# A graph layer on one core: x of blocks and own messages made ahead, rows stored in three half passes, SyncE in program order and fetching one unit in 90

## Chip, core and metric

The kernel runs on one core of a Trainium2 chip. The metric is device time in microseconds (us) of one execution; the time before is the median of three runs. One further execution was profiled; its trace is where every duration below comes from. The engines are called as the profile calls them: PE (matmul) with PEld (its weight load), DVE, ACT, POOL (GpSimd) and SP (SyncE, which here only starts DMAs). L302 is line 302 of the kernel before.

## What is computed

One layer of a graph network on 50,000 nodes of 160 features and 1,650,000 edges, sorted by target. Every node has an edge to itself (`_loop`). In the reference, cut to what matters:

```
src = concatenate([_s, _d, arange(50000)]); dst = concatenate([_d, _s, arange(50000)])   # then sorted by dst, stable
ss, vv = s[src], v[src]                       # gather rows of x by edge
m = (four products of ss, vv with the edge's 4 attributes and W1..W5)
m_agg = segment_sum(m, dst)
h = (m_agg times Ws and Wv)
x = layernorm(x + (x + relu(h)))
```

Since everything up to the ReLU is linear in x for fixed attributes, the kernel sums attribute times x row per target first (four sums of 160 numbers per node, one for each attribute) and multiplies by the combined weights (`BWa`, `BWb`) afterwards.

## The kernel before, in words

**Tiling.** 128 edges are a *unit*, 6 units a *group*, 2 groups a *pair* (12 units), 20 groups a *super-group* (10 pairs). There are 2,086 groups, so 1,043 pairs. The main loop (L755) runs over pairs. For a unit, POOL gathers the 128 rows of x that its edges name (L302, one indirect DMA into a slice of `xg`; the tile `xg` holds a pair's 12 units, and the pool `rows` has 5 such tiles). DVE makes `hot` (which of 32 target slots an edge belongs to, L311) and `ha` (`hot` times each of the four attributes, L314), and PE multiplies `ha` by the gathered rows, accumulating a group in PSUM (L324). ACT copies the sums out (L327).

**After a chunk of 4 groups** (2 pairs) the sums are transposed (`turn`, L559, L562), multiplied by the weights (`apply_weights`, L573) and kept as `hp` (L577). When the last chunk that touches a block of 128 nodes is done, the block is finished: `nodes` loads the block's x and self sums (L589, L593), `own` makes the messages of the nodes to themselves (L607 to L620), `block` adds the chunks' parts (L630, L631), then the layer norm (L175 to L190) and the store (L734). These steps are put off by a fixed number of pairs with `after_pair` (L779 to L786): turn 1, weights and loads 2, own 3, block 4, square root 5, norm 6, send 7.

**Packing.** Self edges needn't be gathered, so from group 60 on (`HEAD`) the kernel reads edges from which they were taken out. It takes them out itself, beside the main loop: the edges are read in packs of 120 rows of 790 edges (`pack`, 17 packs), each row is compacted on DVE (L425 to L504; its self edges' attributes are summed into `mine`, L465), and each row is stored to DRAM by SP, one DMA for its edges (18 KB) and one for its self sums, at addresses held in a table (`row_table`) and loaded into SP registers, ten rows a step (`store`, L513 to L541, loads at L519 and L522). A row's tail is overwritten by the head of the next, so all rows are stored without their head of 32 entries and then all heads: 2 x 12 steps. From super-group 3 on the edges are loaded back from there (L238). The steps of a pack are spread evenly over the pairs up to its due time (L748 to L777), which is pair 19 for the first pack, 69 for the second, and 60 pairs later for each further one.

**Order.** The program is written in this order and a scheduler orders each engine's instructions by its own model, adding the waits. Instructions of an engine, SP's DMAs too, then run in that order. Every DMA of SP signals one of eight semaphores in turn and waits for the one that used it eight DMAs before.

**Fetching by rows.** The kernel has a second way to get a unit's rows, `fetch` (L656), which is empty before since `HELP` is: an engine loads 32 row offsets (`offsets`, made by ACT in `cast`, L258) into registers and starts one DMA of 640 bytes for each, four such batches a unit, at pairs about 7, 5, 4 and 2 ahead of its use. The unit is the last of its pair, and POOL then leaves it out (L301).

Of the kernel before, what the change touches and what calls it, by code (L numbers as in the profile page):

```python
# [38 lines left out]
F32 = mybir.dt.float32  # L39
# [12 lines left out]
NK = 4  # L52
# [14 lines left out]
HELP = {}  # L67
HEAD = 60
# [31 lines left out]
def tile_gnn_resnorm(ctx: ExitStack, tc: tile.TileContext, x, src, dst, attr, W1, W2, W3, W4, W5, Ws, Wv, out, n_edges):  # L100
# [110 lines left out]
    with tc.tile_pool(name="once", bufs=1) as once, tc.tile_pool(name="raw", bufs=2) as rawp, \  # L211
            tc.tile_pool(name="idx", bufs=2) as idxp, tc.tile_pool(name="rows", bufs=5) as rowp, \
            tc.tile_pool(name="far", bufs=3) as farp, \
            tc.tile_pool(name="ops", bufs=3) as op, tc.tile_pool(name="sums", bufs=4) as sump, \
            tc.tile_pool(name="hp", bufs=alive + 4) as hpp, tc.tile_pool(name="node", bufs=3) as np_, \
            tc.tile_pool(name="psC", bufs=1, space=PSUM) as psC, tc.tile_pool(name="psK", bufs=2, space=PSUM) as psK, \
# [10 lines left out]
        dq = nc.sync  # L227
        offsets = {}
# [20 lines left out]
        def cast(loaded):  # L249
            s, n, ri, sf, df, af = loaded  # L250
            if ri is not None:
                rf = rawp.tile([P, 2, P], F32, name="rf")
                nc.scalar.copy(rf[:n], ri[:n])
                sf, df = rf[:n, 0, :], rf[:n, 1, :]
            if HELP:

                ro = rawp.tile([P, P], I32, name="ro")
                nc.scalar.mul(ro[:n], sf, 4.0 * D)  # L258
                offsets[s] = ro
            return s, n, sf, df, af  # L260

        def place(cast_):

            s, n, sf, df, af = cast_
            ng = n // G

            first = idxp.tile([P, SG], F32, name="first")
            nc.vector.tensor_scalar(first[:n], starts[:n], df[:, 0:1], None, op0=ALU.mult)
            nc.tensor.matmul(bank[:, 3, :ng], ones[:n], first[:n, :ng], start=True, stop=True)
            gs = slice(s * SG, s * SG + ng)  # L270
            nc.vector.tensor_scalar(baseB[:, gs], bank[:, 3, :ng], float(N - 1), None, op0=ALU.min)
            for g in range(QG):
                r = slice(g * W, (g + 1) * W)
                for c0, c1, h in ((s * SG // QG, (s * SG + ng) // QG, g),
                                  ((s * SG + ng) // QG, math.ceil((s * SG + ng) / QG), min(g, ng % QG - 1))):
                    if c0 < c1:
                        nc.vector.tensor_scalar(rowid[r, c0:c1],
                                                baseB[r, c0 * QG:c1 * QG].rearrange("p (c g) -> p c g", g=QG)[:, :, h],
                                                pidx[r], float(-g * W), op0=ALU.add, op1=ALU.add)
            pi = bank[:, 1:3, :]  # L280
            nc.tensor.transpose(pi[:, 0, :n], sf, ident[:n, :n])
            nc.tensor.transpose(pi[:, 1, :n], df, ident[:n, :n])
            pk = psK.tile([P, NK, P], F32, name="pk")
            for k in range(NK):
                nc.tensor.transpose(pk[:, k, :n], af[:, :, k], ident[:n, :n])  # L285
            si = idxp.tile([P, P], I32, name="si")
            nc.vector.tensor_scalar(si[:, :n], pi[:, 0, :n], 0.0, float(N - 1), op0=ALU.max, op1=ALU.min)
            rel = idxp.tile([P, P], F32, name="rel")

            nc.vector.scalar_tensor_tensor(  # L290
                rel[:, :n].rearrange("p (g j) -> p g j", j=G), pi[:, 1, :n].rearrange("p (g j) -> p g j", j=G),
                float(N - 1), baseB[:, gs].unsqueeze(2).to_broadcast([P, ng, G]),
                op0=ALU.min, op1=ALU.subtract)
            nc.vector.tensor_reduce(extremes[:, 0, s:s + 1], rel[:, :n], axis=AX.X, op=ALU.min)
            nc.vector.tensor_reduce(extremes[:, 1, s:s + 1], rel[:, :n], axis=AX.X, op=ALU.max)
            return si, rel, pk
# [53 lines left out]
        def row_table(tmp):  # L350

            NT = npacks * RP
            ti = once.tile([1, NT], I32, name="ti")
            at = tmp.tile([1, NT], F32, name="at")
            node = tmp.tile([1, NT], F32, name="node")
            nc.vector.memset(ti, 0)
            with nc.allow_non_contiguous_dma(reason="one number of each row"):
                dq.dma_start(ti[:, :NR], dst[EH:EH + NR * L].rearrange("(o r e) -> o r e", o=1, e=L)[:, :, 0])
            nc.gpsimd.iota(at, pattern=[[L, NT]], base=0, channel_multiplier=0, allow_small_or_imprecise_dtypes=True)
            most, least = math.ceil(EH / degree) + FAR, max(math.floor(EH / degree) - FAR, 0)  # L360
            nc.vector.tensor_scalar(node, ti, float(N), float(-most), op0=ALU.min, op1=ALU.add)
# [5 lines left out]
            nc.vector.tensor_copy(moved.bitcast(I32), node)  # L367
            nc.vector.tensor_copy(node, moved.bitcast(I32))
# [3 lines left out]
            nc.vector.tensor_scalar(moved, ti, float(N), None, op0=ALU.min)  # L372
            nc.vector.tensor_tensor(moved[:, :NR], moved[:, :NR], node[:, :NR], op=ALU.subtract)
            nc.vector.tensor_reduce(strayed[0:1, 0:1], moved[:, :NR], axis=AX.X, op=ALU.min)
            nc.vector.tensor_reduce(strayed[0:1, 1:2], moved[:, :NR], axis=AX.X, op=ALU.max)
            by_round = "o (c i j) -> o c j i"
            nc.vector.tensor_scalar(ti.rearrange("o (c j i) -> o c j i", c=npacks, j=RS),
                                    at.rearrange(by_round, c=npacks, j=RS), float(4 * C), None, op0=ALU.mult)
            nodes_at = moved.bitcast(I32)
            nc.vector.tensor_scalar(nodes_at.rearrange("o (c j i) -> o c j i", c=npacks, j=RS),  # L380
                                    node.rearrange(by_round, c=npacks, j=RS), float(4 * NK), None, op0=ALU.mult)
            return ti, nodes_at

        def pack(c):
# [128 lines left out]
            def store(head, j):  # L513

                m = len(range(j, n, RS))
                if not m:
                    return
                i0 = r0 + j * (RP // RS)
                _, at = nc.values_load_multi_w_load_instructions(  # L519
                    row_at[0:1, i0:i0 + m], engines=[ET.SP], min_val=0, max_val=row_start(NR - 1)[0][1] * 4 * C,  # L520
                    skip_runtime_bounds_check_because="held within bounds")
                _, node = nc.values_load_multi_w_load_instructions(  # L522
                    node_at[0:1, i0:i0 + m], engines=[ET.SP], min_val=0, max_val=row_start(NR - 1)[1][1] * 4 * NK,
                    skip_runtime_bounds_check_because="held within bounds")
                for i in range(m):
                    p = j + i * RS
                    (lo, hi), (nlo, nhi) = row_start(r0 + p)
                    v = nc.s_assert_within(at[i], lo * 4 * C, hi * 4 * C,
                                           skip_runtime_bounds_check_because="held within bounds")
                    e = slice(0, W) if head else slice(W, L)  # L530
                    put(edge_bytes, v, e, C, T["rows"][p:p + 1, e, :])
                    if r0 + p < real:
                        v = nc.s_assert_within(node[i], nlo * 4 * NK, nhi * 4 * NK,
                                               skip_runtime_bounds_check_because="held within bounds")
                        e = slice(0, W // 2) if head else slice(W // 2, W)
                        put(self_bytes, v, e, NK, T["mine"][p:p + 1, 0, e, :])

            def put(mem, at, e, width, what):
                size = (e.stop - e.start) * width * 4
                dq.dma_start(mem[e.start * width * 4:][ds(at, size)].rearrange("(o f) -> o f", o=1),  # L540
                             what.bitcast(U8).rearrange("p e c -> p (e c)"))  # L541
# [4 lines left out]
            for head in (False, True):  # L546
                steps += [partial(store, head, j) for j in range(RS)]
# [36 lines left out]
        def nodes(b):  # L584

            nb, row = rows_of(b)
            cs = of_block[b]
            xt = np_.tile([P, D], F32, name="xt")
# [3 lines left out]
            sa = np_.tile([P, NK], F32, name="sa")  # L592
            dq.dma_start(sa[:nb], selves[0, row.start * NK:row.stop * NK].rearrange("(n k) -> n k", k=NK))  # L593
            rr = np_.tile([P, alive], F32, name="rr")
# [4 lines left out]
            return xt, sa, hot2  # L599

        def own(b, xt, sa, hot2):
# [7 lines left out]
            t = np_.tile([P, D], F32, name="t")  # L609
# [12 lines left out]
            return xt, t, hot2  # L622
# [55 lines left out]
        placed = {0: place(cast(load(0)))}  # L678

        strayed = once.tile([P, 2], F32, name="strayed")  # L680
        nc.vector.memset(strayed, 0.0)
        moved = once.tile([1, npacks * RP], F32, name="moved")
        with tc.tile_pool(name="begin", bufs=1) as beginp:
            row_at, node_at = row_table(beginp)
            weights(beginp, psM)
        packp = later_pools.enter_context(tc.tile_pool(name="pack", bufs=1))
        limit = once.tile([P, 1], F32, name="limit")
        nc.vector.memset(limit, float(KM))
        place_ = once.tile([P, L], F32, name="place")
        nc.gpsimd.iota(place_, pattern=[[1, L]], base=0, channel_multiplier=0, allow_small_or_imprecise_dtypes=True)  # L690
        nc.vector.tensor_scalar(place_, place_, degree, None, op0=ALU.add)
# [6 lines left out]
        nc.vector.memset(counts[:, 1], float(W))  # L698

        nz = math.ceil((row_start(0)[1][1] + W) / P)  # L700
        zeros = once.tile([P, nz * NK], F32, name="zeros")
        nc.vector.memset(zeros, 0.0)
        dq.dma_start(selves[0, 0:P * nz * NK].rearrange("(p f) -> p f", p=P), zeros)
# [11 lines left out]
        def do_weights(c):  # L715
            hps[c] = apply_weights(*parts.pop(c))
            for b in after[c]:
                of_nodes[b] = nodes(b)
# [22 lines left out]

        raws, has = {}, {}
# [11 lines left out]
        done, began = 0, 0  # L754
        for p, (s, g, ng) in enumerate(pairs):  # L755
# [13 lines left out]
            if packs:  # L769
# [8 lines left out]
            if (g + ng) % QG == 0 or g + ng == NG:  # L778
                after_pair(p + 1, do_turn, c, sums)  # L779
                for b in after[c]:  # L780
                    after_pair(p + 3, do_own, b)
# [3 lines left out]
                    after_pair(p + 7, do_send, b)  # L785
# [197 lines left out]
```

## Time and profile before

| what | us |
|---|---|
| median of three runs | 21079.56 |
| lowest, highest | 21071.74, 21093.23 |
| the profiled execution, whole | 16054.09 |
| its span, first to last instruction | 16052.3 |
| POOL busy / PE busy / DVE busy / ACT busy in it | 11845.4 / 12359.3 / 6413.6 / 1574.3 |
| mean granted PE clock in it | 0.687 of full speed |
| gathers: number, mean duration | 12516, 0.946 |
| SP: DMAs that store rows (L540) | 8128 |

The profiled execution is shorter than the timed ones by 5,025 us. The profile is of one execution; a row such as "L302 POOL DMA_INDIRECT xg<-in_x,si x12516 | busy, mean ns | idle before <-who ended it" stands for all instructions of one line. "issue" as the one who ended an idle means that nothing in the profile was waited for. An engine's busy time leaves out the starting of DMAs, so SP has none; its instructions are seen in the timeline and under their lines.

### The profile page before, as it was taken

The page shows a single profiled execution, that of the slowest core. Times are in us where ns is not written, and L with a number is a line of the kernel's source. Part 1 is how long each engine was busy: PE and PEld are TensorE (multiplying, and loading weights), DVE is VectorE, ACT ScalarE, POOL GpSimd, SP SyncE. Part 2 cuts the span into 40 slices and gives each one's busy share as a digit, 9 for nine tenths or more (in the row PEclk, how much of TensorE's full clock was granted, in tenths as well). Part 3 has the DMA queues.
Part 4 walks back from the last instruction along what each step waited for, and adds up shares of the span by engine and source line. Part 5 has one row for each costly group of instructions (what it writes and reads, how often), then busy time and mean ns, then how long its engine had stood idle before and what let it go on. Part 6 is the DMA issues. An engine that isn't in the chain of part 4 may idle for free.

```text
span 16052.3 us, 155475 instructions
## 1 busy us (share of the span) xinstructions
PE 12359.3 (77%) x47011; PEld 8724.9 (54%) x47012; DVE 6413.6 (40%) x15105; ACT 1574.3 (10%) x3873; POOL 11845.4 (74%) x12530
## 2 busy tenths in 40 slices
PE   6176877787777877787778777787878777787887
PEld 4155555555555555555555555555555555555555
DVE  4353434343443434353444434343444434353222
ACT  0011010010101010010101010010101010010100
POOL 7277777777777777777777777777777777777776
PEclk6576667666766667676766667677776766676766
DMA  2133333333333333333333333333333332332322
GB/s 72 34 76 79 77 81 76 79 75 82 75 79 77 78 80 76 80 74 81 75 81 77 78 79 77 80 76 78 75 81 77 78 78 74 77 76 76 75 72 63
DMA packets 813417, 1218.18 MB, mean 76 GB/s; under 512 B 288531, under 2 KB 591540, under 8 KB 808506
## 3 DMA queue, kind: packets, MB, share of 16 engines
q0 software_dynamic: 600768, 1026.11, 26.2%
q1 hardware_dynamic: 211196, 181.54, 4.1%
q8 instruction: 373, 6.11, 0.2%
q14 instruction: 472, 3.87, 0.1%
q10 hardware_dynamic: 608, 0.55, 0.0%
HBM read 1135.43 MB, written 71.86 MB: 75 GB/s over the span
## 4 chain that ended last, share of the span: by engine, by line
POOL 46%; issue 21%; PE 16%; DMA 13%; SPq 3%; DVE 1%; ACT 0%; POOLq 0%; DVEq 0%; ACTq 0%
POOL xg L302 46%; DMA xg<-in_x,si 13%; PE ps L324 7%; PE yx L614 3%; PE yx L613 2%; SPq L540 2%; PE pt L559 2%; PE phb L630 1%; PE phc L573 1%; SPq L522 1%; SPq L519 1%; PE ptx L607 0%; DVE pra L465 0%; DVE prow L504 0%; PE pk L285 0%
## 5 line engine op out<-in xcount | busy, mean ns | idle before, releaser
L302 POOL DMA_INDIRECT xg<-in_x,si x12516 | 11841.1, 946 | 4157.0 <-issue 3561.3
L324 PE MATMUL ps<-xg,ha 128*128 128x160 f32 x25032 | 7383.7, 423 | 3146.7 <-DMA xg<-in_x,si 3097.5
L324 PEld LDWEIGHTS ps<-xg,ha 128*128 128x128 f32 x25032 | 4989.1, 254 | 5478.5 <-DMA xg<-in_x,si 4913.8
L314 DVE TENSOR_TENSOR ha<-hot,pk 128x1536 f32<-128x1536 f32 x1043 | 1826.8, 1752 | 5367.2 <-PE ps L324 5367.2
L465 DVE SCALAR_TENSOR_TENSOR pra<-marks,prow 120x236 bf16<-120x236 f32 (+40 forms) x2924 | 1501.6, 514 | 33.1
L327 ACT COPY A<-ps 128x320 f32<-128x320 f32 x1043 | 443.4, 425 | 6528.1 <-PE ps L324 6503.8
L614 PE MATMUL yx<-BWb,xT 32*128 32x320 f32 x1564 | 1000.3, 735 | 1.6 <-ACT xT L608 1.6
L613 PE MATMUL yx<-BWa,xT 128*128 128x320 f32 x1564 | 960.8, 713 | 0.7 <-ACT xT L608 0.7
L559 PE MATMUL pt<-ident,A 128*128 128x128 f32 (+1 forms) x4172 | 918.2, 371 | 42.8 <-DVE t L620 30.2
L562 ACT COPY at<-pt 128x512 f32<-128x512 f32 (+1 forms) x1044 | 601.4, 580 | 3218.1 <-PE pt L559 3203.9
L630 PE MATMUL phb<-hp,hot 128*128 128x160 f32 x4688 | 892.6, 352 | 0.0
L630 PEld LDWEIGHTS phb<-hp,hot 128*128 128x128 f32 x4688 | 846.6, 236 | 14.9 <-ACT at L562 10.9
L573 PE MATMUL phc<-BWa,at 128*128 128x160 f32 x4176 | 790.9, 341 | 1.0 <-ACT at L562 1.0
L573 PE MATMUL phc<-BWb,at 32*128 32x160 f32 x4176 | 771.4, 327 | 0.0
L559 PEld LDWEIGHTS pt<-ident,A 128*128 128x128 f32 (+1 forms) x4172 | 642.7, 166 | 230.2 <-issue 114.3
L573 PEld LDWEIGHTS phc<-BWa,at 128*128 128x128 f32 x4176 | 736.2, 227 | 7.1 <-ACT at L562 6.6
L573 PEld LDWEIGHTS phc<-BWb,at 32*128 32x128 f32 x4176 | 636.9, 201 | 104.7 <-issue 104.7
L614 PEld LDWEIGHTS yx<-BWb,xT 32*128 32x128 f32 x1564 | 351.3, 278 | 605.7 <-ACT xT L608 300.7
L618 DVE TENSOR_SCALAR t<-yx,sa 128x160 f32<-128x160 f32 x391 | 149.7, 383 | 1193.5 <-PE yx L614 1192.5
L631 DVE TENSOR_TENSOR phb<-phb,t 128x160 f32<-128x160 f32 x391 | 129.8, 332 | 1168.3 <-PE phb L630 972.5
L620 DVE SCALAR_TENSOR_TENSOR t<-yx,sa,t 128x160 f32<-128x160 f32 x1173 | 445.0, 379 | 329.1 <-PE yx L614 323.3
L311 DVE TENSOR_TENSOR hot<-bank,rel 128x384 f32<-128x384 f32 x1043 | 564.1, 546 | 3.5
(148 smaller groups left out, 4547.5 us busy)
## 6 DMA issues: line engine op xcount, KB each, us to landing
xg<-in_x,si POOLq DMA_INDIRECT x12516
selves<-mine SPq DMA_DIRECT2D x4062, 0.2 KB
r<-edges SPq DMA_DIRECT2D x101, 360.0 KB
edges<-prow SPq DMA_DIRECT2D x2033, 17.8 KB
edges<-prow SPq DMA_DIRECT2D x2033, 0.8 KB
xt<-in_x SPq DMA_DIRECT2D x390, 80.0 KB
out<-o SPq DMA_DIRECT2D x390, 80.0 KB
pra<-in_attr SPq DMA_DIRECT2D x16, 1481.2 KB
```

Source lines behind the costliest of these rows:

```text
L302: nc.gpsimd.indirect_dma_start(out=xg[:, j, :], out_offset=None, in_=x, in_offset=bass.IndirectOffsetOnAxis(ap=placed[0][:, u + j:u + j + ...
L311: nc.vector.tensor_tensor(hot[:, :n], slotsP[:, 0:W].unsqueeze(1).to_broadcast([P, n, W]), rel[:, u:u + n].unsqueeze(2).to_broadcast([P, n ...
L314: nc.vector.tensor_tensor(ha[:, :n], hot[:, :n].unsqueeze(2).to_broadcast([P, n, NK, W]), pk[:, :, u:u + n].rearrange("p k u -> p u k").un ...
L324: nc.tensor.matmul(ps[:, j // G, :], ha[:, j].rearrange("p k w -> p (k w)"), xr, start=j % G == 0, stop=j % G == G - 1)
L465: nc.vector.scalar_tensor_tensor(T["waste"][:n, w0:w1], T["marks"][:n, w0 - a:w1 - a], float(w + 1), T["rows"][:n, w0:w1, 2 + k], op0=ALU. ...
L559: nc.tensor.transpose(pt[:f1 - f0, g, :], A[:, i, f0:f1], ident)
L562: evict(at[:, :, :ng].rearrange("f k g w -> f g k w"), pt[:f1 - f0, :ng].rearrange("f g (k w) -> f g k w", w=W))
L573: nc.tensor.matmul(ph[:ng * W], at[:, k, :ng].rearrange("f g w -> f (g w)"), bw[:, k, :], start=i == 0, stop=i == 2 * NK - 1)
L613: nc.tensor.matmul(y[:nb], xT[:, 0, :nb], BWa[:, ks, :], start=True, stop=False)
L614: nc.tensor.matmul(y[:nb], xT[:D - P, 1, :nb], BWb[:, ks, :], start=False, stop=True)
L620: nc.vector.scalar_tensor_tensor(t[:nb], y[:nb, i], sa[:nb, k:k + 1], t[:nb], op0=ALU.mult, op1=ALU.add)
L630: nc.tensor.matmul(ph[:nb], hot2[:r, i, :nb], hp[:r], start=i == 0, stop=i == len(cs) - 1)
```

## The change

1. `HELP` gets SP with a period of 90 units: SP fetches one unit in 90 by rows. ACT makes the offsets of every super-group.
2. `HEAD` goes from 60 to 100 groups, so five super-groups are read unpacked. There are 2,087 groups then and 1,994 rows, still 17 packs; the first is due at pair 39, the second at 89.
3. Rows are stored in three half passes: even rows without regard to what they overwrite, odd rows, then the heads of the even rows. A step loads 20 registers in one instruction, from a table `spots` that interleaves both addresses, and its addresses need no addition. Three empty steps follow each store step.
4. A block's x and self sums are loaded 7 pairs before its last chunk is complete (`ahead`), and its own messages are made 3 pairs before (`own`), not after. Their tiles come from a pool of 7 of each. The send goes from 7 pairs after to 8. The pool `rows` goes from 5 tiles of `xg` to 4.
5. SP's instructions keep the program's order (`manual_schedule`) from the main loop on.
6. The weights, the row table and the zeros (L703) are made within the first two pairs, behind the first placement; packing begins at pair 2.

The diff, cut to its core:

```
-HELP = {}
-HEAD = 60
+HELP = {ET.SP: 90}
+HEAD = 100
...
-            tc.tile_pool(name="idx", bufs=2) as idxp, tc.tile_pool(name="rows", bufs=5) as rowp, \
+            tc.tile_pool(name="idx", bufs=2) as idxp, tc.tile_pool(name="rows", bufs=4) as rowp, \
...
+            tc.tile_pool(name="ahead", bufs=7) as aheadp, \
...
-                i0 = r0 + j * (RP // RS)
-                _, at = nc.values_load_multi_w_load_instructions(
-                    row_at[0:1, i0:i0 + m], engines=[ET.SP], min_val=0, max_val=row_start(NR - 1)[0][1] * 4 * C,
-                    skip_runtime_bounds_check_because="held within bounds")
-                _, node = nc.values_load_multi_w_load_instructions(
-                    node_at[0:1, i0:i0 + m], engines=[ET.SP], min_val=0, max_val=row_start(NR - 1)[1][1] * 4 * NK,
+                ni = RP // RS
+                i0 = (c * RS + j) * 2 * ni
+                _, spot = nc.values_load_multi_w_load_instructions(
+                    spots[0:1, i0:i0 + 2 * ni], engines=[ET.SP], min_val=0,
...
-                    e = slice(0, W) if head else slice(W, L)
-                    put(edge_bytes, v, e, C, T["rows"][p:p + 1, e, :])
+                    put(edge_bytes, v, T["rows"][p:p + 1, :W if head else L, :])
...
-                        e = slice(0, W // 2) if head else slice(W // 2, W)
-                        put(self_bytes, v, e, NK, T["mine"][p:p + 1, 0, e, :])
+                        put(self_bytes, v, T["mine"][p:p + 1, 0, :W // 2 if head else W, :])
...
-            for head in (False, True):
-                steps += [partial(store, head, j) for j in range(RS)]
+
+            for head, j0 in ((False, 0), (False, 1), (True, 0)):
+                for j in range(j0, RS, 2):
+                    steps += [partial(store, head, j), None, None, None]
             return steps + [stored]
...
+        def ahead(b):
+
+            nb, row = rows_of(b)
+            xt = aheadp.tile([P, D], F32, name="xt")
+            dq.dma_start(xt[:nb], x[row, :])
+
+            assert rows_stored[0] == NR or row_start(rows_stored[0])[1][0] >= row.stop
+            sa = aheadp.tile([P, NK], F32, name="sa")
+            dq.dma_start(sa[:nb], selves[0, row.start * NK:row.stop * NK].rearrange("(n k) -> n k", k=NK))
+            return xt, sa
...
-            t = np_.tile([P, D], F32, name="t")
+            t = aheadp.tile([P, D], F32, name="t")
...
+        def do_ahead(b):
+            of_nodes[b] = ahead(b)
...
+        START = 2
+        AHEAD = 7
...
+        for at, bs in zip(complete, after):
+            for b in bs:
+                after_pair(max(at - AHEAD, START - 1), do_ahead, b)
+                after_pair(max(at - AHEAD + 4, START), do_own, b)
+        later_pools.enter_context(tc.manual_schedule(engines={ET.SP}))
         for p, (s, g, ng) in enumerate(pairs):
...
+            if p == START - 2:
+                with ExitStack() as behind, tc.tile_pool(name="begin", bufs=1) as beginp:
+                    for i in first_ones:
+                        behind.enter_context(tc.issue_after(i))
+                    weights(beginp, psM)
+            if p == START - 1:
...
+                    row_table(tablep)
...
-            if packs:
+            if packs and p >= START:
...
-                    after_pair(p + 3, do_own, b)
                     after_pair(p + 4, do_block, b)
                     after_pair(p + 5, do_root, b)
                     after_pair(p + 6, do_store, b)
-                    after_pair(p + 7, do_send, b)
+                    after_pair(p + 8, do_send, b)
```

## Prediction

> **What bounds the kernel now.** I read the page's engine totals first, then the costliest groups, then who waited for whom on POOL, then POOL's instructions one by one, then stretches of time.
>
> ```profile
> PE 12359.3 (77%) x47011; PEld 8724.9 (54%) x47012; DVE 6413.6 (40%) x15105; ACT 1574.3 (10%) x3873; POOL 11845.4 (74%) x12530
> L302 POOL DMA_INDIRECT xg<-in_x,si x12516 | 11841.1, 946 | 4157.0 <-issue 3561.3
> ```
>
> POOL and PE look alike (74% and 77%). What differs is what they wait for. The second line is the whole of POOL's work: 12,516 gathers of 128 rows of x, 946 ns each. The list of waits and a piece of POOL's timeline (start, duration, idle before):
>
> ```profile
> POOL xg L302 <- issue: 3561.3, 11691, 0.3
> POOL xg L302 <- DVE si L287: 309.1, 2, 288.4
> POOL xg L302 <- PE ps L324: 181.8, 597, 0.3
> ...
> PE ps L324 <- DMA xg<-in_x,si: 3097.5, 5424, 9.0
> ```
>
> ```profile
> 8000.53 0.95 POOL L302 DMA_INDIRECT xg<-in_x,si  x1 [0.30 <-issue]
> 8001.78 0.95 POOL L302 DMA_INDIRECT xg<-in_x,si  x1 [0.30 <-issue]
> 8003.03 0.94 POOL L302 DMA_INDIRECT xg<-in_x,si  x1 [0.30 <-issue]
> ```
>
> POOL starts a gather every 1.25 us with an idle of 0.30 us that nobody causes ("issue"; the waits put down to PE are never over 0.3 us, so they are the same 0.30). PE waits 3097 us for gathers; POOL never waits for PE. So POOL's issue is the bound: 12,515 steps x 1.251 us = 15,656 us. The first gather starts at 25.0 us and the last at 16,002.0 us, which is 15,977 us; 321 us are thus no ordinary steps, and 288.4 of them are the one wait above. The stretches around it (busy PE, PEld, DVE, ACT, POOL, clock, DMA):
>
> ```profile
> 400.00:500.00 100.00, 40.40 (x182) 28.29 (x181) 89.23 (x203) 8.80 (x23) 65.32 (x70) 0.62 0.33 80
> 500.00:600.00 100.00, 0.00 (x0) 0.00 (x0) 0.00 (x0) 0.06 (x1) 0.00 (x0) 0.50 0.04 16
> 600.00:700.00 100.00, 0.00 (x0) 0.00 (x0) 0.00 (x0) 0.00 (x0) 0.00 (x0) 0.50 0.02 7
> ```
>
> From 500 to 700 us every engine stands; only SP works, storing the rows of the first pack (L540), because the first super-group that reads them back (the one after the 60 head groups) can't be loaded before. The span is 25 + 15,656 + 321 + 50 (tail after the last gather) = 16,052 us.
>
> SP is the queue that gets the new work. Its stores, with and without an address addition (the first two, then the last two), and its register loads:
>
> ```profile
> 2021.21 0.24 SPq L540 DMA_DIRECT2D edges<-prow  x1
> 2021.62 0.23 SPq L540 DMA_DIRECT2D selves<-mine  x1
> ...
> 2181.88 0.23 SPq L540 DMA_DIRECT2D edges<-prow  x1
> 2182.20 0.23 SPq L540 DMA_DIRECT2D selves<-mine  x1
> ```
>
> ```profile
> L522 SPq TENSOR_LOAD <-moved x408: 967/1890/2746, 438.1 to 14882.7; - x136
> L519 SPq TENSOR_LOAD <-ti x408: 957/1862/2773, 498.8 to 14880.1; - x136
> ```
>
> So one row costs SP 0.40 us with the addition and 0.32 without; loading ten registers 0.96 to 2.77 us, about 1.88 (0.19 per register).
>
> **What the Trainium skill says.** "DMA: Bandwidth & Descriptors", section "Issuing engines are not separate DMA queues": moving DMAs to another engine saves only the issuing sequencer's time. That is what is short here: the DMA share is about 0.3, POOL's step is constant. Same page, "SWDGE vs HWDGE vs iDMA": POOL's DMAs have their descriptors made by software, SP's by hardware. The trace agrees that the prices differ, though not to SP's favour per row: POOL 1.25 us for 128 rows, SP 0.32 for one. "Runtime: NRT & Kernel Launch", section "Instruction fetch mechanics": a register load costs about 200 ns per register even in bulk; the trace has 0.19.
>
> **The change, part by part.**
>
> *Fewer gathers.* One unit in 90 is fetched by SP: 138 units. The larger head (100 groups for 60) drops fewer self loops early and adds one group, 6 units. 12,516 + 6 - 138 = 12,384 gathers, which is also the count in the changed program. 132 x 1.251 = 165 us off the path.
>
> *The first stall.* With 100 head groups, rows are first read back for pair 50 instead of 30, and the first pack has until pair 39 instead of 19. Before, its DVE work ended at 498 us and the load ran at about 760. Pair 50 is gathered at 25 + 50 x 15.0 = 775 us, its load stands at pair 40 (625 us). In the changed DVE order the first pack ends beside pair 24, about 385 us, earlier than before, and its 18 store steps follow in SP's program by pair 39. I take the 288 us as gone; late next is POOL itself. Bounds: 288 to 0.
>
> *Start.* The zeros (an SP store of 11.2 us ahead of the first loads) and the row table move behind the first placement. First gather at 17 instead of 25 us: 8 us (0 to 10).
>
> *x and own messages ahead.* The same DMAs and matmuls, 4 to 7 pairs earlier; PE does the same work. PE loses 78 us of waiting for x, beside POOL's path: 0. Four xg buffers instead of five leave POOL 3 pairs (45 us) ahead of PE instead of 4; before, no POOL wait for PE was over 0.3 us, and PE's longest wait for x, 50 us, goes with the early load: 0, cover being those 45 us. ACT's 105 extra conversions of 120 x 128, at the 0.4 us of its nearest cast, are 42 us on an engine 10% busy: 0.
>
> *SP's new load.* Fetching: 138 units x 4 batches of 32 rows. A batch is 32 x 0.33 = 10.6 us plus 32 registers x 0.2 = 6.4: 17.0 us, 552 of them 9,380 us. Stores: rows go in three half passes instead of four (even, odd, heads of even), 5,979 instead of 8,128 DMAs, without the addition: 306 steps x (19.5 x 0.33 + 20 x 0.2) = 3,200 us. The other 1,300 or so DMAs at 0.43: 560. Sum 13,140 us, 84% of 15,590. Nothing of it is on POOL's path as long as SP keeps up. Bounds by the durations above: rows 0.32 to 0.40, registers 0.10 to 0.28: 10,400 to 16,400 us.
>
> *SP in program order.* Sending block b waits for o of DVE, two pairs after it in the program; behind it queue the next fetches and stores, and PE waits for those rows at the last unit of the helped pair. The last batch stands two pairs before its use, so SP has about 2.9 pairs = 43 us for the 17 us, and POOL another 45 us by its buffers. Locally: in the 29 of each 60 pairs that store, SP has per pair 4 x 17.0 / 7.5 = 9.1 us of fetches, 10.5 / 1.6 = 6.5 of stores, 0.5 of others, 16.1 us against 15.0; it falls 32 us behind, inside the 88, and wins it back in the other 31 pairs (9.6 of 15.0). I take 0.
>
> *Sum.* 17 + 12,383 x 1.251 + 32 (slow steps as before) + 50 = 15,590 us of span, 15,592 against the profiled execution's own 16,054: -462, -2.9%. The median shown, 21,080, lies 5,025 us above that execution, and no view tells why. If it is slower gathers (0.40 us on each of 12,516), the saving is 132 x 1.65 + 288 + 8 = 514; if all is stretched alike, 607; if something constant is added, 462. I take 520: **20,560 us** (20,450 to 20,700 over the three).
>
> **Rivals.**
> - *SP becomes the bound (slower).* Place: the fetch loop, its register loads and 17,664 row DMAs, and the wait for DVE's o ahead of them. At the upper bound SP's 16,400 us, with the head and tail some 16,450, exceed 16,054; stretched to the median's scale 21,500 us (21,120 to 21,900). It decides from where SP's sum passes 16,000: 2,860 us more over 23,640 rows, 0.12 us each, or as much per register. For: 84% by middle prices and no allowance for order waits; in the trace of before SP stood 4,617 us for buffers alone (L593). Against: those waits were for work that the early load decouples, and in the slower timed executions SP may have more time per pair.
> - *SP lags in the store stretches only*, or the first pack still is late: gives back 100 to 450 us: 20,700 to 21,100.
> - *The timed executions aren't bound by POOL's issue.* Then fewer gathers give nothing, the stall's 288 remain: 20,790. For: the unexplained 5,025 us. Against: nothing in the trace is near a second bound, PE waits for POOL.
>
> **How the numbers follow.** Forecast 0.56. SP as the bound 0.26, slower. Partial loss 0.13: 0.08 faster, 0.05 within 0.2%. Other bound 0.05, faster. 0.2% (42 us) is about what a measurement of this kernel can tell from no change. Faster 0.56 + 0.08 + 0.05 = 0.69, same 0.05, slower 0.26. The range from 20,400 to 21,300 leaves out some 0.16 of the slow case above and 0.03 below.
>
> **What would show it.** Right: 12,384 gathers at 1.25 us and no POOL wait over a few us; all stretches between 400 and 800 us as full as later ones; SP's waits for DVE but no wait of PE's ps for xr over 45 us; register loads of 32 at about 6 us. Wrong: POOL waiting for PE's ps by tens of us in the half of each pack that stores, PE waiting for DMA xr, row DMAs on SP more than 0.4 us apart, or a POOL stall at pair 50.

## The result, and the profile after

The changed kernel takes 22,746.95 us (22,727.13 to 22,755.42), the kernel before 21,085.08: ratio 1.0787, 95% interval 1.0769 to 1.0806. It is slower; the prediction said 20,560 and faster.

The runs below were taken in sets, each with the kernel before beside it, and before took about 21,080 us in some sets and about 16,080 in others; "at 21,080" and "at 16,080" say which kind a set was, and the execution on which the prediction rests (16,054) was of the short kind, the times shown beside it of the long kind.

The page of the changed kernel (engine totals and the costliest group):

```profile
PE 10816.8 (48%) x47031; PEld 8448.5 (37%) x47032; DVE 6647.2 (29%) x15106; ACT 1599.2 (7%) x3981; POOL 11755.0 (52%) x12398
...
L304 POOL DMA_INDIRECT xg<-in_x,si x12384 | 11750.7, 949 | 10875.2 <-PE ps L326 5060.5
```

The gathers are fewer by 132, as forecast, and each takes 0.949 us where it took 0.946. But POOL now idles 10,875 us before them where it idled 4,157, and it is PE that ends most of that (6,380 us over all of PE's lines). The list of waits:

```profile
POOL xg L304 <- PE ps L326: 5060.5, 343, 69.7
DVE ha L316 <- remote: 3827.5, 216, 55.1
...
POOL xg L304 <- issue: 3606.0, 11723, 18.4
...
PE pt L564 <- DVE t L629: 1622.9, 187, 52.9
```

("remote": no releaser was found.) The "issue" share (0.30 us at each gather) is what it was. New are 5,060 us in which POOL waits for a free xg tile, in 343 waits of up to 70 us, and PE's wait for own messages of DVE (`t`), 30 us in the trace of before. SP's own waits:

```profile
SPq L671 <- ACT xT L617: 995.2, 9, 126.0
SPq L671 <- ACT ro L260: 293.4, 6, 129.5
SPq L737 <- DVE o L190: 271.6, 25, 57.0
```

All the waits listed for SP together are 2,201 us; before they were 10,938 in the first trace and 9,388 in a trace at 21,080 (run e1 below). SP is occupied for the other 20,524 us of 22,725: it is full. The row DMAs, by tile (duration in ns: least, median, most):

```profile
L676 SPq MOVE xr<-in_x x17664: 1/29/1420, 7.5 to 22506.2; - x199
L676 SPq DMA_DIRECT2D xr<-in_x x17664: 1/228/1422, 7.6 to 22506.2; - x199
```

The medians are the ones expected (0.03 + 0.23 us and a little between), the ends are not. A piece of the timeline shows what the ends are (start, duration, engine; the 19.53 is POOL's idle time before that gather):

```profile
8036.04 7.73 SPq L676 DMA_DIRECT2D xr<-in_x  x24
...
8043.70 0.95 POOL L304 DMA_INDIRECT xg<-in_x,si  x1 [19.53 <-PE ps L326]
...
8049.42 0.00 SPq L543 DMA_DIRECT2D selves<-mine  x1
8049.96 0.94 POOL L304 DMA_INDIRECT xg<-in_x,si  x1 [0.30 <-issue]
8050.14 0.71 SPq L543 DMA_DIRECT2D edges<-prow  x1
8050.87 0.00 SPq L543 DMA_DIRECT2D selves<-mine  x1
8051.21 0.95 POOL L304 DMA_INDIRECT xg<-in_x,si  x1 [0.30 <-issue]
8051.59 0.72 SPq L543 DMA_DIRECT2D edges<-prow  x1
...
8055.90 0.29 PEld L326 LDWEIGHTS ps<-xg,ha 128*128 128x128 f32 x1 [1.24 <-issue]
8056.22 0.95 POOL L304 DMA_INDIRECT xg<-in_x,si  x1 [0.30 <-issue]
8056.59 0.00 SPq L543 DMA_DIRECT2D edges<-prow  x1
8056.61 0.43 PE L326 MATMUL ps<-xg,ha 128*128 128x160 f32 x1 [1.70 <-issue]
```

From 8,049 us on SP's DMAs stand 0.72 or about 1.4 us apart, not 0.33: the MOVE ahead of each DMA (left out of this view) and the DMA can each wait for a step of about 0.7 us. PE's loads and matmuls move in the same steps here and wait for nothing that is shown ("issue"). POOL keeps its 1.25 us. While POOL stood, just before, 24 rows took SP 7.73 us, 0.32 each. Counted over the trace, about 6,600 of SP's instructions stand 0.68 to 0.74 us after the one before, 4,350 stand 1.38 to 1.48 us; in the first trace of before these are 15 and 24.

The steps go with POOL's gathers. The trace has 174 gaps of over 15 us between two gathers; from 3 us after the last gather to the next one they hold 4,319 us, and SP's instructions stand in steps for 112 us of that, 3%, although SP starts 4.5 instructions per us there and PE 2.6. Over the whole trace it is 10,757 us of 22,725.

The stretches that answer to the first stall of before:

```profile
400.00:500.00 100.00, 37.47 (x160) 28.73 (x160) 72.84 (x166) 5.12 (x14) 43.57 (x46) 0.64 0.17 46
500.00:600.00 100.00, 54.30 (x236) 42.04 (x237) 31.81 (x47) 6.68 (x17) 61.59 (x65) 0.65 0.22 57
600.00:700.00 100.00, 55.26 (x241) 43.83 (x240) 24.83 (x42) 7.58 (x19) 61.18 (x65) 0.65 0.23 62
```

The standstill is gone: POOL is busy for 44 to 62 us of each hundred, against 52% over the whole trace.

### The profile page after: what moved, and what is told of

It is laid out like the page before. It is cut to its first block, busy times and chain, and to the rows that moved or that the text cites. A ratio compares the mean times of both kernels' runs of the same rounds, so it can differ in the third digit from the quotient of the medians.

```text
span 22725.4 us, 182874 instructions
## 1 busy us (share of the span) xinstructions
PE 10816.8 (48%) x47031; PEld 8448.5 (37%) x47032; DVE 6647.2 (29%) x15106; ACT 1599.2 (7%) x3981; POOL 11755.0 (52%) x12398
## 5 line engine op out<-in xcount | busy, mean ns | idle before, releaser
L326 PE MATMUL ps<-xg,ha 128*128 128x160 f32 x24768 | 5022.2, 355 | 2907.0 <-issue 2541.1
L326 PEld LDWEIGHTS ps<-xg,ha 128*128 128x128 f32 x24768 | 4469.0, 233 | 3341.0 <-issue 2910.2
L564 PE MATMUL pt<-ident,A 128*32 128x128 f32 (+1 forms) x4174 | 990.8, 384 | 2646.8 <-DVE t L629 1622.9
L616 PE MATMUL ptx<-ident,xt 128*128 128x128 f32 (+2 forms) x782 | 280.1, 358 | 3459.9 <-ACT xT L617 1649.1
L564 PEld LDWEIGHTS pt<-ident,A 128*32 128x32 f32 (+1 forms) x4174 | 566.6, 160 | 3104.6 <-issue 2018.2
L471 DVE SCALAR_TENSOR_TENSOR pra<-marks,prow 120x236 bf16<-120x236 f32 (+40 forms) x2924 | 1503.2, 514 | 357.0 <-remote 131.3
L616 PEld LDWEIGHTS ptx<-ident,xt 128*128 128x128 f32 (+2 forms) x782 | 104.5, 134 | 3668.8 <-ACT xT L617 1726.1
L639 PE MATMUL phb<-hp,hot 128*128 128x160 f32 x4694 | 1070.7, 394 | 711.7 <-issue 532.7
L639 PEld LDWEIGHTS phb<-hp,hot 128*128 128x128 f32 x4694 | 973.7, 266 | 801.5 <-issue 593.7
L578 PE MATMUL phc<-BWa,at 128*128 128x160 f32 x4176 | 891.2, 370 | 555.0 <-issue 350.5
L578 PE MATMUL phc<-BWb,at 32*128 32x160 f32 x4176 | 877.9, 359 | 183.5 <-issue 120.6
```

The lines of the kernel that those rows point to most:

```text
L326: nc.tensor.matmul(ps[:, j // G, :], ha[:, j].rearrange("p k w -> p (k w)"), xr, start=j % G == 0, stop=j % G == G - 1)
L471: nc.vector.scalar_tensor_tensor(T["waste"][:n, w0:w1], T["marks"][:n, w0 - a:w1 - a], float(w + 1), T["rows"][:n, w0:w1, 2 + k], op0=ALU. ...
L564: nc.tensor.transpose(pt[:f1 - f0, g, :], A[:, i, f0:f1], ident)
L578: nc.tensor.matmul(ph[:ng * W], at[:, k, :ng].rearrange("f g w -> f (g w)"), bw[:, k, :], start=i == 0, stop=i == 2 * NK - 1)
L639: nc.tensor.matmul(ph[:nb], hot2[:r, i, :nb], hp[:r], start=i == 0, stop=i == len(cs) - 1)
```

## Experiments

Theory A: SP is saturated by the fetch. Rivals: SP's program order (C), four xg tiles or early own messages (D). What the runs raised later is theory E: the order that the scheduler gave to DVE. Where an expectation needs its own form of A, or a rival B, it spells it out.

**First set (before 21,070.79 us).**

`e1`: the kernel before, unchanged.

> The kernel before, unchanged. The trace on which the prediction rests spans 16,052 us, 5,025 us less than the timed median; the changed kernel's trace spans what its timed runs span. All theories: time 21,080, ratio 1.00. Theory A (an instruction of SP takes about 0.7 us in its slow stretches whenever POOL makes gather descriptors in executions of the timed kind): the trace of this run spans about 21,080 us, and SP's row stores stand 0.7 us or more apart for much of it, where the first trace had 0.32 to 0.40. Theory B (the 0.7-us steps come from the change itself): SP's row stores are 0.32 to 0.40 us apart here too, and gathers or something else than SP take the other 5,000 us.

Measured: 21,090.18, ratio 1.0009 (1.0000 to 1.0019), span of the trace 21,058. Its gathers and its list of waits:

```profile
L302 POOL DMA_INDIRECT xg<-in_x,si x12516 | 11876.4, 949 | 9108.2 <-issue 3567.3
```

```profile
POOL xg L302 <- PE ps L324: 2545.4, 208, 135.5
```

A gather costs 0.949 us, hardly more than in the short trace (0.946). POOL's waits other than "issue" are 5,540 us here and were 595 there; PE ends 3,505 of them, for 1,640 no releaser was found, and the first stall is 345. SP's instructions move in the 0.7-us steps (about 2,660 and 1,440 of the two kinds), and SP is occupied for 11,670 us where the same 23,736 instructions took 5,115 in the short trace. Theory A's premise holds. In the stall, in which POOL stands, 1,263 instructions of SP follow each other without one such step. PE too waits longer: 2,974 us for a block's x (`xt`), 78 in the short trace.

`e2`: the changed kernel without its fetch. `e3`: the changed kernel with SP in the scheduler's order. `e4`: before with the fetch.

```
e2  -HELP = {ET.SP: 90}        +HELP = {}
e3  -        later_pools.enter_context(tc.manual_schedule(engines={ET.SP}))
e4  (before) -HELP = {}  +HELP = {ET.SP: 90};  name="rows", bufs=5 -> bufs=4
```

> The changed kernel without its fetch by rows: HELP is empty again, so POOL gathers all 12,522 units; early loads, half passes, program order, larger head and four xg tiles stay. Theory A (SP is saturated by its 17,664 row DMAs and their register loads): the loss is gone, 20,600 to 20,850 us (before less the 288 us of the first stall and a few more), gathers again without long gaps. Rival C (SP's program order and its wait for o hold up the stream): 22,300 to 22,700, gaps in the gathers stay. Rival D (four xg tiles or the earlier own messages stall POOL on PE): 22,300 to 22,700 too, with POOL waiting for PE's ps while SP idles.

> The changed kernel with SP's instructions in the scheduler's order in place of the program's; all else as changed, the fetch too. Theory A (SP is saturated by the fetch): within 1.5% of the changed kernel, 22,400 to 23,100 us. Rival C (program order is what costs): 20,600 to 21,200.

> The kernel before with the fetch alone added (one unit in 90 by SP, in the scheduler's order, and four xg tiles for five so that the offsets fit). Theory A: the fetch costs as much as the whole change or more, since the stores here are 8,128 DMAs with address additions and the first stall stays: 22,700 to 24,000 us. Rivals C and D (program order, early own messages): 20,900 to 21,200; rival D by four tiles alone: slower than before, with POOL waiting for PE and SP free.

Measured: e2 20,420.46, ratio 0.9691 (0.9675 to 0.9707); e3 22,796.00, 1.0812 (1.0794 to 1.0830); e4 25,641.71, 1.2165 (1.2145 to 1.2186). The loss needs the fetch: without it the rest of the change gains 650 us, more than the 220 to 470 expected, and PE's wait for `xt` falls to 236 us; with it alone before loses 4,571, again more than expected. Program order is not the loss (49 us between e3 and the changed kernel): rival C falls. Four tiles and early own messages are in e2 too, which is faster than before, so rival D is not the loss by itself. But adding the fetch also made the scheduler order DVE anew (the table further down), so these runs don't yet tell SP's load from DVE's order.

**Second set (before 16,082.50 us).** Which part of the fetch costs, and do the steps need POOL?

```
e5  no values_load;  xbytes[ds(v, 4 * D)]  ->  xbytes[a:a + 4 * D], a fixed
e6  32 row DMAs  ->  dma_start(xr[i * nr:(i + 1) * nr, :], x[r0:r0 + nr, :])
e7  for j: gpsimd.indirect_dma_start(xg[:, j, :] ...)  ->  dq.dma_start(xg[:, :m, :], x[r0:r0 + m * P, :] ...)
e8  (e2, in the loop over pairs)  + for _ in range(16): nc.scalar.copy(idle, none_)
```

> The changed kernel with the 17,664 row DMAs at fixed addresses: no register loads and no MOVE in the fetch, so the rows fetched are not those that the edges name. SP's instructions fall from 50,484 to about 32,200, its row DMAs stay. Theory A1 (the number of SP's instructions costs, whatever they are): the loss halves, 21,400 to 21,800 us. Theory A2 (the row DMAs themselves cost): 22,300 to 22,800. Undisturbed sums (0.25 us a row) say 20,250.

> The changed kernel with one DMA of 32 neighbouring rows in place of each 32 row DMAs, without their register loads, so the rows fetched are not those that the edges name. The 138 units still need no gather. All theories in which the fetch's load on SP costs: 20,150 to 20,400 us, the run without fetch less up to 138 gathers. If what costs is the last unit's wait for another source than POOL: 21,500 or more.

> The changed kernel with POOL's 12,384 gathers left out: one plain DMA of SP for each pair brings as many neighbouring rows of x, so the rows are not those that the edges name; bytes, fetch, stores and all the rest stay. Theory A (SP and the other engines step at 0.7 us only while POOL makes gather descriptors): no such steps, row DMAs 0.32 us apart throughout, 11,500 to 13,500 us, set by PE. Theory B (the steps come from the many small DMAs of SP): the steps stay for half of SP's time, over 18,000 us.

> The changed kernel without its fetch (20,420 us) plus 16 copies of a single number for each pair on ACT, 16,704 in all, on which nothing waits. ACT is busy 8%; a copy is 0.2 to 0.3 us by ACT's smallest rows, 3 to 5 us of a pair's 19.5. Theory A3 (every instruction of any engine costs while POOL gathers; 36,600 more by the fetch cost 2,300 us, 0.063 us each): about 21,450 us. Rival (only SP's instructions or DMAs do): 20,400 to 20,600.

Measured: e5 15,623.83 (0.9716, 0.9699 to 0.9732), e6 15,676.82 (0.9747, 0.9731 to 0.9763), e7 13,636.75 (0.8485, 0.8471 to 0.8499), e8 18,133.95 (1.1276, 1.1257 to 1.1294). The set was at 16,080, where the steps hardly occur, so the expectations, made for 21,080, aren't met and aren't refuted. e8 is a miss: busy tenths of ACT and POOL in 40 slices,

```profile
ACT  4888688757101010101010101010101010101000
POOL 7112611463777777777777777777777777777777
```

the scheduler put nearly all copies into the first quarter, among ACT's real work, and POOL stood behind them; later POOL runs at its usual pace. It says nothing on the steps.

**Third set (before 16,093.21 us).** The changed kernel, e2 and two of the others again (e11 as e5, e12 as e7).

> The changed kernel itself, once more. The kernel before has taken two times: about 21,080 us beside the first runs, 16,080 us beside the last four. Where before is at 16,080 us, theory A (SP goes slow only where the 0.7-us steps occur, and the trace of before at 16,052 us has none) says 15,600 to 15,750 us, ratio 0.970 to 0.980, the prediction's 15,590; a rival by which SP's 13,000 us or so of work is too much in any case says 16,500 or more. Where before is at 21,080 us: 22,750 us again.

> The changed kernel without its fetch, once more. Where before is at 16,080 us: POOL bound, 12,522 gathers x 1.251 + 70, about 15,750 us, so that the fetch's 138 units are worth 100 to 170 us there. Where before is at 21,080 us: 20,420 us again.

> The changed kernel with its row DMAs at fixed addresses (no register loads and no MOVE in the fetch, other rows than the edges name). Where before is at 16,080 us: 15,620 us again. Where before is at 21,080 us: if the number of SP's instructions costs, half of the loss, 21,400 to 21,800 us; if the DMAs do, 22,300 to 22,800.

> The changed kernel with one plain DMA of SP for each pair in place of POOL's gathers (neighbouring rows of x, not those that the edges name). Where before is at 16,080 us: 13,640 us again. Where before is at 21,080 us: if the steps come only while POOL makes descriptors, no steps and 13,640 us here too; if they are the state of the whole core, steps and over 16,000 us.

Measured: the changed kernel 15,981.68 (0.9932, 0.9915 to 0.9948), without fetch 15,860.89 (0.9857, 0.9841 to 0.9873), fixed addresses 15,633.90 (0.9715, 0.9699 to 0.9731), plain loads 13,646.72 (0.8481, 0.8467 to 0.8496). At 16,080 the change is 0.7% faster, and SP is not the bound. Against plain loads POOL's gathers cost 2,335 us here (the changed kernel less the run without gathers). The run without fetch was expected at 15,750, 100 to 170 us above the one with it; measured, it is 121 below. The row DMAs of the changed kernel here, from the view of their line:

```profile
L676 SPq MOVE xr<-in_x x17664: 29/29/38, 7.4 to 15781.4; - x199
L676 SPq DMA_DIRECT2D xr<-in_x x17664: 227/228/2202, 7.5 to 15781.5; - x199
```

The medians are those of 21,080, and every MOVE keeps to it (29 to 38 ns). SP's work, its span less its waits, is 15,977 - 5,808 = 10,169 us, half of the 20,524 that the same 50,484 instructions took above.

But 15,982 isn't the predicted 15,590, nor within the 15,600 to 15,750 expected. Of its waits:

```profile
PE pt L564 <- DVE t L629: 1391.6, 213, 45.1
POOL xg L304 <- PE ps L326: 416.3, 491, 21.5
```

and PE's timeline at one of the longest:

```profile
2496.19 1.35 PE L326 MATMUL ps<-xg,ha 128*128 128x160 f32 x8
2542.38 1.09 PE L564 MATMUL pt<-ident,A 128*128 128x128 f32 x4 [44.84 <-DVE t L629]
```

PE stands 45 us because `pt`, `yx` and three others share two PSUM tiles (the pool `psM`), and `yx` is only freed when DVE has made `t` from it. DVE is not idle then: from 2,456 to 2,550 us it works on the pack (L432 to L471) and waits for 7 us in all. POOL, ahead by its buffers, stands 21.5 us of these 45. That is theory E: the scheduler put the pack's work into clumps on DVE, and own messages behind them. Counted in DVE's order after the first 60 pairs, the part of a pack's DVE instructions that stands in clumps of over 30 between two `ha`, the longest clump, and PE's wait for `t` at 16,080:

| program | in clumps | longest | PE waits for t, us | POOL's delay in gaps, us |
|---|---|---|---|---|
| before | 3% | 31 | 30 | 333, of which 288 the first stall |
| no fetch | 23% | 54 | 29 | 128 |
| fixed addresses | 34% | 57 | 362 | 66 |
| changed | 66% | 129 | 1,392 | 411 |
| half the fetch (next set) | 54% | 139 | 1,014 | 525 |

(The last column is what the gaps between gathers hold beyond 1.251 us each. At 21,080 the programs have the same order on DVE; e4, before with the fetch alone, has 68% in clumps and a wait for `t` of 1,505 us there, before itself 75.)

**Fourth set (before 16,058.18 us).** Every second fetch left out, and e5 and e7 once more (e14, e15), to have them at 21,080, which the set wasn't.

```
e13  -                first += period      +                first += 2 * period
```

> The changed kernel with every second fetch left out: SP fetches one unit in 180, 69 units, 8,832 row DMAs. Where before is at 21,080 us: if the loss is proportional to SP's load, half of the 2,320 us between the changed kernel and the one without fetch, 21,550 to 21,620 us; if it is a saturation of SP (nothing lost until its sum fills the span), 20,450 to 20,900. Where before is at 16,080 us: between 15,860 (no fetch) and 15,980, or 15,780 if the 21 us that a pack loses there go with the load.

> The changed kernel with its row DMAs at fixed addresses (no register loads and no MOVE in the fetch, other rows than the edges name). Where before is at 21,080 us: if the number of SP's instructions costs, about half of the loss, 21,400 to 21,800 us; if the DMAs do, 22,300 to 22,800. Where before is at 16,080 us: 15,620 again.

> The changed kernel with one plain DMA of SP for each pair in place of POOL's gathers (neighbouring rows of x, not those that the edges name). Where before is at 21,080 us: if the 0.7-us steps come only while POOL makes descriptors, no steps and 13,640 us; if they are the state of the whole core, steps and over 16,000 us. Where before is at 16,080 us: 13,640 again.

Measured: half the fetch 16,142.36 (1.0053, 1.0037 to 1.0070), fixed addresses 15,600.55 (0.9715, 0.9699 to 0.9731), plain loads 13,643.54 (0.8494, 0.8480 to 0.8508). Half of SP's load is slower, against its own before, than the whole of it and than none, which no form of the expectation had, though SP waits 9,518 us in it. So at 16,080 the shortfall doesn't go with SP's load. It goes with the clumps of the table in the main: all programs with over half in clumps lose 400 to 525 us, those with less under 130 apart from the first stall. But half the fetch has a smaller part in clumps and a shorter wait for `t` than the whole and still the larger delay, so the table doesn't give its size.

**Fifth set (before 21,071.52 us).** DVE in program order as well: with the fetch, without, and with fixed addresses.

```
-        later_pools.enter_context(tc.manual_schedule(engines={ET.SP}))
+        later_pools.enter_context(tc.manual_schedule(engines={ET.SP, ET.DVE}))
```

> The changed kernel with DVE in program order too, so that at most 15 of a pack's instructions stand between two ha on DVE, where the scheduler put up to 68. Where before is at 16,080 us: theory E (the 410 us of POOL's stalls there come from DVE's clumps of pack work, behind which own messages hold PE's buffers) says 15,560 to 15,650 us, the prediction's time; if they come from SP's load, 15,950 or more. Where before is at 21,080 us: if SP's saturation costs there, still over 22,000 us.

> The changed kernel without the fetch and with DVE in program order. Where before is at 16,080 us: 12,522 gathers x 1.252 + 60 = 15,740 us, 100 to 170 above the same with the fetch. Where before is at 21,080 us: 20,000 to 20,500, the best of all there.

> The changed kernel with DVE in program order and with its row DMAs at fixed addresses (no register loads and no MOVE in the fetch, other rows than the edges name). Where before is at 16,080 us: the same as with register addresses within 30 us if DVE's order was the whole difference between 15,980 and 15,620; 100 us or more below it if SP's loads cost by themselves. Where before is at 21,080 us: if the number of SP's instructions costs, 21,000 to 21,800 us; if the DMAs do, 22,000 to 22,800.

Measured: 21,456.58 (1.0187, 1.0170 to 1.0204); 19,420.89 (0.9222, 0.9207 to 0.9238); 19,838.45 (0.9418, 0.9402 to 0.9434). (The 68 of the first expectation counts a repeated instruction once.) Three things follow, all at 21,080.

First, the fetch costs 21,457 - 19,421 = 2,036 us with DVE in program order in both. With fixed addresses 418 of that remain, and the MOVEs and register loads, 18,200 instructions of SP that move no byte, make 1,618 us, four fifths. (The 418 are net of the 138 gathers that the fetch saves, and fixed addresses also read other rows, so the split is not a clean one.) So the number of SP's instructions costs, more than the DMAs do. All three times lie below what was expected, since I had not counted on what DVE's order gives at 21,080. The way by which a full SP delays the rest is seen in PE's waits for DMAs: 2,741 us in all with the fetch, 142 without. Half of it is for blocks of x that SP loads late (with the fetch, then without; with fixed addresses it is 1.0):

```profile
PE ptx L616 <- DMA xt<-in_x: 1354.2, 83, 46.9
...
PE ptx L616 <- DMA xt<-in_x: 3.5, 1, 3.5
```

Second, DVE's program order gains 22,747 - 21,457 = 1,290 us with the fetch and 20,420 - 19,421 = 1,000 without. The waits of the run with fetch:

```profile
POOL xg L304 <- PE ps L326: 4267.0, 349, 60.8
...
PE pt L564 <- DVE t L629: 244.0, 102, 9.3
```

PE's wait for `t` fell from 1,623 to 244 us; POOL's for PE from 5,061 to 4,267. Without the fetch the wait for `t` was small already (350 us, now 295); there PE's waits for ACT fell, from 3,912 to 2,829 us, and those for DMAs, from 1,027 to 142. So the gain is one of DVE's order as a whole; that the clumps make it is shown for neither. SP is as full as before: its waits are 2,084 us of 21,452. The steps are still there (about 7,250 and 4,150 of the two kinds).

Third, the version without the fetch and with DVE in program order beats both kernels: 7.8% below before. Its waits:

```profile
POOL xg L304 <- PE ps L326: 2248.7, 274, 17.2
```

It wasn't run at 16,080. What holds it above POOL's own pace is PE again, which ends 2,812 of POOL's 3,851 us of waits other than "issue", though SP waits 8,768 us: PE stands 4,521 us with no releaser shown, of which the first trace of before has 0.2.

## Why the prediction was wrong, step by step

- *The trace's prices as prices of the timed executions.* This step failed, and it decided the sign. The prediction saw the 5,025 us between its trace and the median, called them "slower gathers" or "stretched alike", and let all prices stand. The gathers were not slower (0.946 to 0.949 us in every trace). SP's instructions were: SP's sum, put at 13,140 us with 10,400 to 16,400 as its bounds, is 20,524 in the timed executions. The largest term is the rows of the fetch: 0.33 us was taken for each, and on average 0.74 passes there from a row's MOVE to the instruction after its DMA, 13,100 us for 17,664. The argument "in the slower timed executions SP may have more time per pair" had the sign wrong.
- *SP's new load, as prices.* At 16,080 the sum was too high, not too low: 10,169. A row is 0.323 us (0.33 taken), but 32 registers load in 2.13 us where 6.4 was taken, and 20 in 1.46 where 4.0 was: 552 x (32 x 0.323 + 2.13) + 306 x (19.5 x 0.33 + 1.46) + 560 = 9,860. The price per register that the loads of ten give in the trace of before (1.89 us, 0.19 each) doesn't carry over; the Trainium skill's 200 ns a register ("Runtime: NRT & Kernel Launch", section "Instruction fetch mechanics"), which the same page gives for the runtime's loads from HBM, compares with 0.067 for 32 and 0.073 for 20 here.
- *"Nothing of it is on POOL's path as long as SP keeps up".* The condition failed at 21,080, held at 16,080. The rival "SP becomes the bound" named the place rightly and its price too low: 21,500 for 22,747. It put the limit at 0.12 us more for each row; it was 0.41 more, since a row's two instructions can cost a step each. Of the prediction's signs of being wrong, POOL's waits for PE by tens of us (up to 69.7) and row DMAs over 0.4 us apart came; PE's wait for xr hardly did (184 us).
- *Fewer gathers*: 12,384 of 0.949 us, as said. What they are worth at 21,080 was not measured apart; POOL has 3,851 us of waits other than "issue" there even in the fastest run.
- *The first stall*: gone, as said. At 21,080 it is 345 us in before, and the longest wait of POOL in the changed kernel is 69.7.
- *Start*: first gather at 10.4 us for 24.3; 14 us for the 8 forecast.
- *x and own messages ahead, four tiles: 0.* Wrong, and unseen: PE's wait for `t` is 1,392 us at 16,080 and 1,623 at 21,080, against 30 in the first trace. Its cover, "45 us of buffers", held less than that: a wait of PE of 44.8 us stopped POOL for 21.5. (That no wait of POOL for PE was over 0.3 us before is also misread: its list has five for `ptx` of up to 12.1.) I looked at where the steps stand in the program and not at the order that the scheduler made of them for DVE. That this makes 15,982 out of 15,590 at 16,080 is argued from the table above, where the delays follow the clumps in the main and not SP's load; DVE in program order was only run at 21,080. At nothing the prediction also put what the early load of x gains; at 21,080 PE's wait for it is 2,974 us before and 236 in the change without fetch.
- *SP in program order: 0.* Right: 49 us between e3 and the changed kernel, of 22,750.
- *Issuing engines* (the Trainium skill, "DMA: Bandwidth & Descriptors", section "Issuing engines are not separate DMA queues"): moving the DMAs moved only the sequencer's time, as the section says. POOL got 173 us (138 x 1.25), SP paid 35,900 instructions.

What stays open: what makes a set one of 21,080 or of 16,080, and what the 0.7-us steps are. The five sets of experiments ran on five different chips, the two at 21,080 on two of them and the three at 16,080 on the other three; so a difference between chips is a candidate that no run tested. Within a trace at 21,080 SP's steps stop when the gathers stop (above); but gathers alone don't make them, since at 16,080 the same gathers go without. All three runs with plain loads in their place fell into sets at 16,080. Nor was the half dose or a rising number of instructions on another engine run at 21,080.

## What to carry to other kernels

Ask of a profiled execution first whether it is one of the timed ones: where its own time is far from the median, profile the kernel again before any price is taken from it, and look which engine's prices differ, since the difference needn't lie where the bound is. Work moved to an idle queue is to be counted in instructions, not bytes: 138 gathers of 1.25 us were bought with 35,900 instructions, and about four fifths of their cost at 21,080 went with the addresses. And where a scheduler orders an engine, compare its order after the change with the one before: work of an off-path engine that stands in clumps can reach the bound through the buffers that it frees late, as the 45 us above did.

## What the runs showed of the hardware, unexpected

- Two kinds of sets: the kernel before took 21,034 to 21,134 us in some and 16,054 to 16,097 in others. POOL's gather is the same in both (0.946 to 0.949 us); SP's instructions go in steps of about 0.70 us for part of the time in the first (10,757 of 22,725 us in the changed kernel), hardly ever in the second (about 100 of its 50,484 instructions).
- At 21,080 SP's steps stop when POOL's gathers stop: 112 us of steps in 4,319 us of gaps, and none in the 345 us of the first stall, where SP starts 1,263 instructions.
- At 21,080 SP's instructions without a byte to move aren't free: leaving out 18,200 of them gains 1,618 us, 0.09 us each of the whole kernel's time, though a MOVE is 0.029 us by its median.
- A register load of 32 neighbouring registers takes 2.13 us, of 20 takes 1.46, of ten 0.96 to 2.77.
